# Last buckets of two graph layers: gathered rows and one-hots in place of stored matrices

## The chip, the cores and the metric

One core of a Trainium2 chip runs one program. The metric is device time in microseconds (us) of one execution, the median over runs. Engines are named as in the profile: PE (matrix products) with PEld (its weight loads), DVE (vector), ACT (scalar), POOL (GpSimd), SP (which here only issues DMAs). A bank is one of PE's eight accumulator banks, 128 partitions by 512 f32.

## The reference

A graph of 8192 nodes (32 features each, `x`) and 262144 edges, sorted by target `dst`, so a node has 32 edges on average. Four layers, each followed by a residual sum and a normalization over the 32 features:

```python
def layernorm(x): return (x - mean(x)) / sqrt(var(x) + 1e-5)
def segsum(msg): return segment_sum(msg, dst, 8192)

x = layernorm(x + segsum(einsum('ei,eio->eo', x[src], weight[edge_type])))   # layer 0, 64 types
x = layernorm(x + segsum(x[src] * edge_weight[:, None]))                     # layer 1
x = layernorm(x + segsum(x[src]))                                            # layer 2
x = layernorm(x + L3(x, src, dst, edge_attr_4, edge_attr_32))                # layer 3
```

Layer 3 makes a small matrix for each edge from its 32 attributes (two dense steps) and multiplies it into the source row.

## The kernel before

All the work is in `raw_layers`, written engine by engine with marks and waits: `PE.after(mark)` makes the engine wait for a mark, `V.mark(ins)` makes one. Every engine runs its instructions in the order in which they are written there. Edges lie in 2048 tiles of 128 (edge on partition), eight tiles to a *group*, so 256 groups; nodes lie in 64 *buckets* of 128. Because edges are sorted, group g meets only a window of 128 nodes that begins near node 32 g; four groups hold about one bucket.

**Layer 0 (L607 to L681)** gathers, for each edge, a row of `ytab` (one row per node and edge type, 64 MB, made in the prologue) with an indirect DMA from POOL (`gathers`, `indirect`, L387), one per tile. A one-hot of the target within the group's window (`one_hot`, L508) sums the rows on PE into a bank (L662, in three bf16 parts); `windows` (L483) adds the shifted windows of neighbouring groups into buckets, and `normalize` (L452) ends eight buckets at a time.

While layer 0 waits for its gathers, `matrices(i)` (L553, one call per group or so) builds what layers 1 and 2 need: for each of 256 steps, the adjacency of 32 nodes as dense blocks. DVE makes two one-hots and a weighted copy of the first (L562, L564, L567), PE multiplies them (L576), ACT moves the result out as bf16 counts and f32 weights (L581, L582), and SP stores 1 MB into `famat` (weighted, layer 1) and 0.5 MB into `fcmat` (counts, layer 2).

**Layers 1 and 2 (L756 to L779)** read these matrices back: layer 1 in 32 chunks of two buckets, layer 2 in 16 chunks of four; each chunk is one DMA of 8.4 MB (64 KB for each partition) into one of two buffers. `bring(n)` (L692) issues the load of a chunk once its buffer is free, that is once the products two chunks before have read it. The loop over chunks does, on PE: the 64 products of the chunk (L761 or L764), then `turn` (L733) for the chunk before, which adds partial sums into buckets and, every eight buckets, calls `normalize`; in layer 2 also `self_part` (L720), node-wise products for layer 3. Layer 2 begins after layer 1's last normalization. Layer 2's results are stored to `fxtab` (L480), 1 MB.

**Layer 3 (L842 to the end)** gathers from `fxtab`, again one indirect DMA per tile on POOL, once the stores to `fxtab` have landed. SP's DMAs are all in one queue, and POOL's in another.

Of the kernel before, what the change touches and what calls it, by code (L numbers as in the profile page):

```python
# [101 lines left out]
AW = 41200  # L102


@with_exitstack
def in_order(ctx: ExitStack, tc, x, a, w0, w1, b1, w2, si, keep):


    nc = tc.nc
    dram = ctx.enter_context(tc.tile_pool(name="fdram", bufs=1, space=DRAM))  # L110
    const = ctx.enter_context(tc.tile_pool(name="fconst", bufs=1))
    pool = ctx.enter_context(tc.tile_pool(name="fps", bufs=1, space=PSUM))
    m = {}
    m["ytab"] = dram.tile([N * R, D], FP, name="fytab")
    m["xtab"] = dram.tile([N, D], FP, name="fxtab")
    m["hist"] = dram.tile([GG + 4, 8, 16], FP, name="fhist")

    m["amat"] = dram.tile([P, NU * 512], FP, name="famat")
    m["cmat"] = dram.tile([P, NU * 512], BF, name="fcmat")

    def sb(name, shape, dt=FP):
        m[name] = const.tile(shape, dt, name="f_" + name)

    sb("x_b", [P, NB, D])
    for name, dt in (("src", I32), ("row", I32), ("rel", FP)):
        sb(name, [P, TT], dt)
    sb("ident", [P, P])
    sb("shift", [P, 10 * WS])
    sb("iota_s", [P, P])
    sb("iota_b", [P, 16], BF)  # L130
    sb("stack", [P, D])
    sb("upper", [P, P])
    sb("small", [P, 8])
    sb("lnf", [P, 3, LC * D])
    sb("lns", [P, 4, LC])
    sb("arena", [P, AW])
    m["bank"] = pool.tile([P, 8, 512], FP, name="bank")
    res = keep.tile([P, NB, D], FP, name="x_a")
    m["x_a"] = res
    bad = keep.tile([1, 1], I32, name="bad")  # L140
    with tc.tile_critical():
        raw_layers(tc, x, a, w0, w1, b1, w2, si, m, bad)
    return res, bad


def raw_layers(tc, x, a, w0, w1, b1, w2, si, m, bad):
# [7 lines left out]
    ytab, xtab, hist, amat, cmat = (m[k] for k in ("ytab", "xtab", "hist", "amat", "cmat"))  # L154
# [294 lines left out]
    x_st = Landing(tc, "st_x")  # L449
    ln_last = [None]  # L450

    def normalize(l, c, acc, pm, x_in, x_out, x3=None):  # L452


        ds = slice(c * LC, (c + 1) * LC)
        y, yc, sq = (lnf[:, k].rearrange("p (d f) -> p d f", f=D) for k in range(3))
        V.after(pm, ln_last[0])
        read = own(V, V.e.tensor_add(y, acc.rearrange("p (d f) -> p d f", f=D), x_in[:, ds, :]))  # L458
        own(V, V.e.tensor_reduce(lns[:, 0], y, AX.X, OP.add))
        own(V, V.e.tensor_scalar(lns[:, 1], lns[:, 0], 1.0 / D, None, op0=OP.mult))  # L460
        vm = V.mark(V.e.tensor_sub(yc, y, lns[:, 1, :, None].to_broadcast([P, LC, D])))
        A.after(vm)
        V.after(A.mark(A.e.activation(sq, yc, AF.Square)))
        A.after(V.mark(V.e.tensor_reduce(lns[:, 2], sq, AX.X, OP.add)))
        V.after(A.mark(A.e.activation(lns[:, 0], lns[:, 2], AF.Sqrt, bias=eps, scale=1.0 / D)))
        own(V, V.e.reciprocal(lns[:, 3], lns[:, 0]))
        xo = x_out[:, ds, :]
        ln_last[0] = V.mark(V.e.tensor_tensor(xo, yc, lns[:, 3, :, None].to_broadcast([P, LC, D]), op=OP.mult))
        if x3 is not None:

            r1, r2 = y, sq
            V.after(ln_last[0])
            own(V, V.e.tensor_copy(x3[:, ds, 0:D], xo))
            own(V, V.e.tensor_sub(r1, xo, x3[:, ds, 0:D]))
            own(V, V.e.tensor_copy(x3[:, ds, D:2 * D], r1))
            own(V, V.e.tensor_sub(r2, r1, x3[:, ds, D:2 * D]))
            ln_last[0] = V.mark(V.e.tensor_copy(x3[:, ds, 2 * D:], r2))
        if l == 2:
            S.after(ln_last[0])
            x_st.add(S.e.dma_start(xtab.rearrange("(d p) f -> p d f", p=P)[:, ds, :], xo))  # L480
        return read

    def windows(c, acc, free):  # L483

        d0 = c * LC
        todo = []
        for j in [0, 1, 2, 3, -2, -1, 4]:
            lo, hi = 0, LC
            while 4 * (d0 + lo) + j < 0:
                lo += 1  # L490
            while 4 * (d0 + hi - 1) + j >= GG:
                hi -= 1
            if lo < hi:
                todo.append((j, lo, hi))
        wv = win.rearrange("p (d j) f -> p d j f", j=4)
        PE.after(*free)
        for n, (j, lo, hi) in enumerate(todo):
            g0 = 4 * (d0 + lo) + j
            ins = PE.e.matmul(acc[:, lo * D:hi * D].rearrange("p (d f) -> p d f", f=D),
                              shift[:, P - WS * j:2 * P - WS * j], wv[:, g0 // 4:g0 // 4 + hi - lo, g0 % 4, :],  # L500
                              start=(n == 0), stop=(n == len(todo) - 1))
        return PE.mark(ins)

    def ready(c):

        return min(GG, 4 * (LC * (c + 1) - 1) + 5)
# [46 lines left out]
    def matrices(i):  # L553
# [3 lines left out]
        if i % WB == 0:  # L557
            n = min(WB * 16, CB * 16 - i * 16)
            V.after(now(V))
            own(V, V.e.tensor_copy(w_ps[:, 0:n], meta_w.rearrange("p n k -> p (n k)")[:, i * 16:i * 16 + n]))  # L560
# [3 lines left out]
        V.e.tensor_tensor(oh_l[:, b], iota[:, None, :].to_broadcast([P, 16, P]),  # L564
                          meta_l[:, pp, k0:k0 + 16, None].to_broadcast([P, 16, P]), op=OP.is_equal)
        wo = (i % WB) * 16
        vm = V.mark(V.e.tensor_tensor(oh_k[:, b, :, 1, :], oh_k[:, b, :, 0, :],  # L567
                                      w_ps[:, wo:wo + 16, None].to_broadcast([P, 16, 64]), op=OP.mult))
        PE.after(vm)
        for q in range(4):  # L570
            bk = [2 + (2 * units[0] + h) % 5 for h in range(2)]
            PE.after(*(bank_free[b5] for b5 in bk))
            for j in range(4):
                for h in range(2):
                    hs_ = slice(64 * h, 64 * h + 64)
                    ins = PE.e.matmul(bank[:, bk[h], :].rearrange("p (c s j) -> p c s j", s=64, j=4)[:, :, :, j],  # L576
                                      oh_l[hs_, b, 4 * q + j, :], oh_k[hs_, b, 4 * q + j], start=True, stop=True)
            pm = PE.mark(ins)
            A.after(pm, st_ld[b].mark() if q == 0 and st_ld[b].n else None)
            for h in range(2):  # L580
                A.e.activation(st_c[:, b, q, h], bank[:, bk[h], 0:256], AF.Copy)  # L581
                bank_free[bk[h]] = am = A.mark(A.e.activation(st_a[:, b, q, h], bank[:, bk[h], 256:512], AF.Copy))  # L582
# [3 lines left out]
        st_ld[b].add(S.e.dma_start(amat[:, 2048 * i:2048 * (i + 1)], st_a[:, b].rearrange("p u h c -> p (u h c)")))  # L586
# [57 lines left out]
    for g in range(GG + 2):  # L644
        if g >= 2 and (g - 2) % per == per - 1:
            vm = bank_out((g - 2) // per)
            while done < NB // LC and ready(done) <= g - 1:
                acc = bank[:, (g - 2) // per % 2, 0:LC * D]
                agg_free[(g - 2) // per % 2] = vm = normalize(0, done, acc, windows(done, acc, (vm,)), x_a, x_b)
                done += 1  # L650
# [15 lines left out]
        if g >= FIRST:  # L666
            upto = min(CB, (g - FIRST + 1) * CB // (GG - FIRST - 4))
# [13 lines left out]
    z = cut(NB, D)  # L681
    zx = cut(2, P)
    end = (now(PE), now(V), now(A), *stored)
# [5 lines left out]
    seq = [(1, c) for c in range(32)] + [(2, c) for c in range(16)]  # L689
    land = {}  # L690

    def bring(n):  # L692
        if n < len(seq):
# [3 lines left out]
            if l == 1:  # L697
                land[n] = m_ld[b].add(S.e.dma_start(buf[b], amat[:, c * 16384:(c + 1) * 16384]))
            else:
                land[n] = m_ld[b].add(S.e.dma_start(buf[b].bitcast(BF), cmat[:, c * 32768:(c + 1) * 32768]))  # L700

    bring(0)
    bring(1)
# [14 lines left out]
    own_part = [None]  # L718

    def self_part(j):  # L720
        xv = x_b[:, 4 * j:4 * j + 4, :].rearrange("p d f -> p (d f)")
        u = j % 2
        if j == 0:
# [5 lines left out]
        PE.after(A.mark(A.e.activation(zx[:, u], bank[:, 4 + u, 0:P], AF.Copy)), zf[1 - u])  # L729
        V.after(PE.mark(PE.e.matmul(bank[:, 6, 0:P], zx[:, u], sis, start=True, stop=True)))  # L730
        zf[u] = V.mark(V.e.tensor_add(z[:, 4 * j:4 * j + 4, :].rearrange("p d f -> p (d f)"), bank[:, 6, 0:P], xv))

    def turn(l, c, n, am):  # L733
# [10 lines left out]
        if d0 + nb == LC:  # L744
            out_free[o] = normalize(l, c * nb // LC, bank[:, 2 + o, 0:LC * D], pm, x_b if l == 1 else x_a,
                                    x_a if l == 1 else x_b, x3 if l == 1 else None)
            outs[0] += 1

    for n, (l, c) in enumerate(seq):
        b = n % 2  # L750
        nn = 256 if l == 1 else 512
        if n == 32:
            turn(*pend)
            pend = None
            PE.after(ln_last[0])
# [19 lines left out]
        if l == 2 and c >= 3 and c % 2 == 1:  # L775
            self_part(c - 3)
            self_part(c - 2)
# [3 lines left out]
    self_part(NB // 4 - 2)  # L781
    self_part(NB // 4 - 1)
# [43 lines left out]
    G.after(x_st.mark())  # L826
# [15 lines left out]
    def fetch_rows(q):  # L842

        if q < NQ:
            G.after(quad.get(q - AHEAD, {}).get("w"))
            rows[q // 2] = gathers(xtab, src, q // 8, q % 8 * 4, 4)
# [68 lines left out]
    for q in range(NQ + LAG3 + 2):  # L915
# [69 lines left out]
        if 0 <= c < NQ and c % 2 == 1:  # L985
# [9 lines left out]
            while done < NB // LC and ready(done) <= g + 1:  # L995
                k, wp = w_bank()
                acc = bank[:, 3 + 2 * k, 0:LC * D]
                w_free[k] = normalize(3, done, acc, windows(done, acc, (w_free[k], gm)), z, x_a)
                done += 1
# [471 lines left out]
```

## Time and profile before

| | us |
|---|---|
| median of 10 runs | 6447.62 (6442.39 to 6453.61) |
| the profiled execution | 6447.4 |
| its span | 6445.0 |

Busy time over the span: PE 4779.0, PEld 3442.4, DVE 4362.1, ACT 1755.4, POOL 3975.1 us. The page's strip of 40 slices of 161 us each shows the stages; a digit is a busy share in tenths:

```
PE   7356666565656565644446879999999999999998
DVE  4278878888888897830000017888878888888887
POOL 2677777777777777730000017777777777777775
DMA  9468777777777777889999961111111111111111
```

The first one or two slices are the prologue, up to slice 17 it is layer 0, then layers 1 and 2 until slice 23, and then layer 3.

How the views are read: a group of instructions is `line engine operation out<-in`, with its count and busy time, and what ended the engine's idle time before it. In the chain of waits each step is followed back to what released it, so a piece named DMA is time in which the next step waited for that transfer. POOL's and SP's DMAs are issued by the engine and carried out by 16 DMA engines which all queues share; a DMA queue's row has its packets, MB, and the time that its packets took as a share of 16 engines. The trace also keeps a record of each packet, with queue, size and duration.

### The profile page before, as it was taken

How to read it: one execution, taken by the hardware profiler on the slowest of the kernel's cores; microseconds unless marked ns; L12 is line 12 of the kernel's file. 1: busy time of each engine (PE TensorE's matmuls, PEld its weight loads, DVE VectorE, ACT ScalarE, POOL GpSimd, SP SyncE). 2: the span in 40 equal slices, each digit the busy share in tenths (PEclk: the TensorE clock that was granted, in tenths of full speed). 3: DMA queues.
4: the chain of work that ended last, by engine and by line, in shares of the span. 5: the costliest groups of instructions: out<-in, count | busy, mean ns of one | idle time of the engine just before them, and what ended most of it. 6: DMA issues, size and time to landing. Idle time of an engine off the chain costs nothing.

```text
span 6445.0 us, 89476 instructions
## 1 busy us (share of the span) xinstructions
PE 4779.0 (74%) x34036; PEld 3442.4 (53%) x34036; DVE 4362.1 (68%) x9246; ACT 1755.4 (27%) x4886; POOL 3975.1 (62%) x4174
## 2 busy tenths in 40 slices
PE   7356666565656565644446879999999999999998
PEld 3155555555555555532223446666666666666665
DVE  4278878888888897830000017888878888888887
ACT  5345444454545454510000001111111111111111
POOL 2677777777777777730000017777777777777775
PEclk7577878887878787877777879999999999999999
DMA  9468777777777777889999961111111111111111
GB/s 350 160 140 182 181 169 187 176 187 174 178 174 190 171 190 164 187 276 432 431 425 407 387 242 28 28 28 28 28 28 28 28 28 28 28 28 29 28 29 21
DMA packets 290756, 999.51 MB, mean 155 GB/s; under 512 B 99021, under 2 KB 175886, under 8 KB 250638
## 3 DMA queue, kind: packets, MB, share of 16 engines
q1 hardware_dynamic: 155742, 916.89, 40.1%
q0 software_dynamic: 134144, 73.67, 13.1%
q8 instruction: 272, 4.46, 0.3%
q10 hardware_dynamic: 432, 3.15, 0.2%
q14 instruction: 166, 1.36, 0.1%
HBM read 521.39 MB, written 471.99 MB: 154 GB/s over the span
## 4 chain that ended last, share of the span: by engine, by line
PE 27%; DMA 26%; DVE 20%; POOL 18%; issue 7%; ACT 1%; POOLq 0%; SPq 0%; DVEq 0%; ACTq 0%
POOL f_arena L387 18%; PE bank L932 9%; DMA f_arena<-fytab,f_row 8%; DMA f_arena<-famat 8%; PE bank L923 7%; DMA f_arena<-fxtab,f_src 5%; DVE f_arena L564 5%; DMA f_arena<-fcmat 3%; PE bank L576 3%; DVE f_arena L562 2%; PE bank L761 2%; DVE f_arena L567 2%; DVE f_arena L509 2%; PE bank L764 2%; PE bank L899 2%
## 5 line engine op out<-in xcount | busy, mean ns | idle before, releaser
L387 POOL DMA_INDIRECT f_arena<-fxtab,f_src x2048 | 1950.2, 952 | 1645.0 <-PE bank L730 1021.3
L387 POOL DMA_INDIRECT f_arena<-fytab,f_row x2048 | 1957.0, 956 | 652.4 <-issue 550.7
L576 PE MATMUL bank<-f_arena 64*128 64x128 f32 x16384 | 1349.3, 331 | 759.6 <-DVE f_arena L567 736.0
L576 PEld LDWEIGHTS bank<-f_arena 64*128 64x128 f32 x16384 | 1272.2, 240 | 827.2 <-DVE f_arena L567 774.2
L932 PE MATMUL bank<-f_arena 128*128 128x344 f32 x4096 | 1314.1, 463 | 0.0
L581 ACT ACTIVATE f_arena<-bank 128x256 bf16<-128x256 f32 x2048 | 868.3, 425 | 1228.8 <-PE bank L576 1172.9
L923 PE MATMUL bank<-f_arena 65*128 65x256 f32 x4096 | 1022.0, 393 | 75.6 <-DVE f_arena L967 75.2
L923 PEld LDWEIGHTS bank<-f_arena 65*128 65x128 f32 x4096 | 770.1, 193 | 429.2 <-DVE f_arena L967 147.7
L932 PEld LDWEIGHTS bank<-f_arena 128*128 128x128 f32 x4096 | 800.0, 195 | 360.5 <-issue 33.8
L907 ACT ACTIVATE f_arena<-bank,f_arena 64x512 f32<-64x512 f32 x512 | 351.0, 686 | 2123.7 <-PE bank L899 2117.3
L582 ACT ACTIVATE f_arena<-bank 128x256 f32<-128x256 f32 x2048 | 882.8, 432 | 0.0
L509 DVE TENSOR_TENSOR f_arena<-bank,f_rel 128x512 f32<-128x512 f32 (+1 forms) x768 | 660.5, 860 | 55.8 <-ACT f_arena L541 44.4
L564 DVE TENSOR_TENSOR f_arena<-bank,f_arena 128x2048 f32<-128x2048 f32 x256 | 586.5, 2291 | 8.7
L967 DVE TENSOR_TENSOR f_arena<-bank,f_arena 128x256 f32<-128x256 f32 x1536 | 552.6, 417 | 0.0
L761 PE MATMUL bank<-f_arena,f_x_b 128*32 128x256 f32 x4096 | 295.8, 460 | 338.4 <-DMA f_arena<-famat 338.4
L458 DVE TENSOR_TENSOR f_lnf<-bank,f_x_b 128x256 f32<-128x256 f32 x8 | 3.4, 425 | 611.0 <-PE bank L741 611.0
L761 PEld LDWEIGHTS bank<-f_arena,f_x_b 128*32 128x32 f32 x4096 | 146.0, 132 | 477.0 <-DMA f_arena<-famat 312.7
L863 DVE TENSOR_TENSOR f_arena<-f_arena 128x192 f32<-128x192 f32 x256 | 93.5, 365 | 412.1 <-DMA f_arena<-fxtab,f_src 410.7
L963 DVE TENSOR_TENSOR f_arena<-bank,f_arena 128x512 f32<-128x512 f32 x512 | 349.6, 683 | 0.0
L662 PE MATMUL bank<-f_arena 128*128 128x96 bf16 x2048 | 142.5, 217 | 268.5 <-DVE f_arena L629 268.4
L562 DVE TENSOR_TENSOR f_arena<-bank,f_arena 128x1024 f32<-128x1024 f32 x256 | 312.0, 1219 | 1.1
L624 DVE TENSOR_SCALAR bank<-f_arena 128x256 int32<-128x256 int32 x256 | 107.9, 422 | 301.1 <-DMA f_arena<-fytab,f_row 300.4
(133 smaller groups left out, 3763.4 us busy)
## 6 DMA issues: line engine op xcount, KB each, us to landing
famat<-f_arena SPq DMA_DIRECT2D x256, 1024.0 KB
fcmat<-f_arena SPq DMA_DIRECT2D x256, 512.0 KB
fytab<-f_arena SPq DMA_DIRECT2D x64, 1024.0 KB, 11.4
f_arena<-fytab,f_row POOLq DMA_INDIRECT x2048
f_arena<-fxtab,f_src POOLq DMA_INDIRECT x2048
f_arena<-laid_ea SPq DMA_DIRECT2D x64, 512.0 KB, 3.6
f_arena<-laid_ea SPq DMA_DIRECT2D x64, 64.0 KB
f_arena<-laid_xT ACTq DMA_DIRECT2D x1, 1024.0 KB, 8.3
```

What stands on the lines that cost most here:

```text
L387: return G.e.indirect_dma_start(out=dest, out_offset=None, in_=table, in_offset=bass.IndirectOffsetOnAxis(ap=ix, axis=0))
L509: return V.e.tensor_tensor(o, iota[:, None, :].to_broadcast([P, n, P]), rel[:, t:t + n, None].to_broadcast([P, n, P]), op=OP.is_equal)
L562: own(V, V.e.tensor_tensor(oh_k[:, b, :, 0, :], iota[:, None, 0:64].to_broadcast([P, 16, 64]), meta_k[:, pp, k0:k0 + 16, None].to_broadcas ...
L564: V.e.tensor_tensor(oh_l[:, b], iota[:, None, :].to_broadcast([P, 16, P]), meta_l[:, pp, k0:k0 + 16, None].to_broadcast([P, 16, P]), op=OP ...
L576: ins = PE.e.matmul(bank[:, bk[h], :].rearrange("p (c s j) -> p c s j", s=64, j=4)[:, :, :, j], oh_l[hs_, b, 4 * q + j, :], oh_k[hs_, b, 4 ...
L581: A.e.activation(st_c[:, b, q, h], bank[:, bk[h], 0:256], AF.Copy)
L582: bank_free[bk[h]] = am = A.mark(A.e.activation(st_a[:, b, q, h], bank[:, bk[h], 256:512], AF.Copy))
L761: ins = PE.e.matmul(bank[q * D:(q + 1) * D, b, 0:256].rearrange("p (u h j) -> p u h j", h=2, j=4), x_b[:, s, :], mv[:, s], start=(s < 4), ...
L907: quad[q + h] = dict(h=A.mark(A.e.activation(hs[0:64, (q + h) % 4], bank[64 * h:64 * h + 64, 2, :], AF.Relu, bias=b1_s[64 * h:64 * h + 64])))
L923: ins = PE.e.matmul(wp[:, t, :], hs[0:65, q % 4, t * P:(t + 1) * P], w2_s[0:65], start=True, stop=True)
L932: ins = PE.e.matmul(bank[:, g % 2, 0:MW], oh[:, c % NO, t, :], p[:, c % NP, t, :], start=(c % 2 == 0 and t == 0), stop=(c % 2 == 1 and t = ...
L967: ins = V.e.tensor_tensor(pq[:, :, 128 + 64 * mm:192 + 64 * mm].rearrange("p t (o i) -> p t o i", i=8), wp[:, :, 192:256].rearrange("p t ( ...
```

## The change

Layer 1's last 10 buckets and layer 2's last 4 are no longer computed from matrices. Layer 1 has 27 chunks and layer 2 has 15. For the rest, groups 214 to 255 in layer 1 and 238 to 255 in layer 2, POOL gathers the source rows from the result of the layer before (42 x 8 and 18 x 8 indirect DMAs), DVE scales them by the edge weight in layer 1, and PE sums them with one-hots. For that, every layer's result goes to a table of its own in DRAM. `matrices` makes 240 steps instead of 256, and the weighted half only in the first 216. Each chunk's load is issued as eight DMAs of 8 KB for each partition.

The helpers take a first bucket and a count in place of a number of eight buckets, `normalize` stores its result in layers 0, 1 and 2, and `windows` can read a ring of 24 groups:

```diff
+HB = {1: 10, 2: 4}
+MADE = {l: CB - 4 * HB[l] for l in (1, 2)}
-    m["xtab"] = dram.tile([N, D], FP, name="fxtab")
+    m["xtabs"] = [dram.tile([N, D], FP, name=f"fxtab{l}") for l in range(3)]
...
-        if l == 2:
+        if l < 3:
             S.after(ln_last[0])
-            x_st.add(S.e.dma_start(xtab.rearrange("(d p) f -> p d f", p=P)[:, ds, :], xo))
+            x_st[l].add(S.e.dma_start(xtabs[l].rearrange("(d p) f -> p d f", p=P)[:, ds, :], xo))
...
+        both = i < MADE[1]
...
-        vm = V.mark(V.e.tensor_tensor(oh_k[:, b, :, 1, :], oh_k[:, b, :, 0, :],
-                                      w_ps[:, wo:wo + 16, None].to_broadcast([P, 16, 64]), op=OP.mult))
+        if both:
+            vm = V.mark(V.e.tensor_tensor(oh_k[:, b, :, 1, :], oh_k[:, b, :, 0, :],
+                                          w_ps[:, wo:wo + 16, None].to_broadcast([P, 16, 64]), op=OP.mult))
...
-            upto = min(CB, (g - FIRST + 1) * CB // (GG - FIRST - 4))
+            upto = min(MADE[2], (g - FIRST + 1) * MADE[2] // (GG - FIRST - 4))
...
-    z = cut(NB, D)
+    HG = {l: 4 * (NB - HB[l]) - 2 for l in (1, 2)}
+    RING = 24
+    hoh = cut(3, 4, P)
+    hx = cut(4, GT, D)
+    hwin = cut(RING, D)
+    ew = cut(TT - T1)
+    z = row.bitcast(FP).rearrange("p (d f) -> p d f", f=D)
...
-    seq = [(1, c) for c in range(32)] + [(2, c) for c in range(16)]
+    chunks = {1: (NB - HB[1]) // 2, 2: (NB - HB[2]) // 4}
+    seq = [(l, c) for l in (1, 2) for c in range(chunks[l])]
...
-            if l == 1:
-                land[n] = m_ld[b].add(S.e.dma_start(buf[b], amat[:, c * 16384:(c + 1) * 16384]))
-            else:
-                land[n] = m_ld[b].add(S.e.dma_start(buf[b].bitcast(BF), cmat[:, c * 32768:(c + 1) * 32768]))
+            for k in range(8):
+                o = buf[b][:, 2048 * k:2048 * (k + 1)]
+                if l == 1:
+                    land[n] = m_ld[b].add(S.e.dma_start(o, amat[:, c * 16384 + 2048 * k:c * 16384 + 2048 * (k + 1)]))
+                else:
+                    land[n] = m_ld[b].add(S.e.dma_start(o.bitcast(BF), cmat[:, c * 32768 + 4096 * k:c * 32768 + 4096 * (k + 1)]))
     bring(0)
+    ew_in = load(S, "ld_ew", ew, a["ew"][:, T1:])
     bring(1)
```

The self parts go to a list and run one chunk after the normalization that they need, in the banks of their transposes instead of a bank that both share. What is new is the gathering, the sums, and their turn at the end of each chunk:

```diff
+    def h_fetch(l, g):
+        if g >= GG:
+            return
+        k = count["got"] % 4
+        count["got"] += 1
+        G.after(x_st[l - 1].mark() if g == HG[l] else None, hx_free[k], hl.get((l, g - 2), (0, None))[1])
+        for t in range(GT):
+            mk = h_ld[k].add(indirect(hx[:, k, t, :], xtabs[l - 1][:, :], src[:, g * GT + t:g * GT + t + 1]))
+        hl[l, g] = k, mk
+
+    def h_sums(l, g0, n):
+        PE.after(h6_free[0])
+        for g in range(g0, g0 + n):
+            k, landed = hl[l, g]
+            V.after(landed)
+            if l == 1:
+                V.after(ew_in)
+                V.e.tensor_tensor(hx[:, k], hx[:, k], ew[:, g * GT - T1:(g + 1) * GT - T1, None].to_broadcast([P, GT, D]), op=OP.mult)
+            for hh in range(2):
+                r = count["oh"] % 3
+                count["oh"] += 1
+                V.after(hoh_free[r])
+                PE.after(V.mark(one_hot(hoh[:, r], g * GT + 4 * hh, 4)))
+                for t in range(4):
+                    ins = PE.e.matmul(bank[:, 6, (g - g0) * D:(g - g0 + 1) * D], hoh[:, r, t, :], hx[:, k, 4 * hh + t, :],
+                                      start=(hh == 0 and t == 0), stop=(hh == 1 and t == 3))
+                hoh_free[r] = hx_free[k] = PE.mark(ins)
+            h_fetch(l, g + 4)
+        V.after(now(PE))
...
+    def h_turn(l, upto):
+        while h_at[l] < upto:
+            n = min(4, upto - h_at[l])
+            h_sums(l, h_at[l], n)
+            h_at[l] += n
+            d = h_done[l]
+            nd = min(4, NB - d)
+            if nd and ready(d + nd) <= h_at[l]:
+                acc = bank[:, 6, 256:256 + nd * D]
+                h6_free[0] = finished(l, d, nd, acc, windows(d, nd, acc, (h6_free[0],), hwin, RING))
+                h_done[l] += nd
 
     for n, (l, c) in enumerate(seq):
...
-        if n == 32:
-            turn(*pend)
-            pend = None
-            PE.after(ln_last[0])
+        if c == 0:
+            if l == 2:
+                turn(*pend)
+                pend = None
+                h_turn(1, GG)
+                PE.after(ln_last[0])
+            h_at[l], h_done[l] = HG[l], NB - HB[l]
+            for k in range(4):
+                h_fetch(l, HG[l] + k)
...
         if pend:
             turn(*pend)
-        if l == 2 and c >= 3 and c % 2 == 1:
-            self_part(c - 3)
-            self_part(c - 2)
+        for j in z_todo:
+            self_part(j)
+        z_todo[:], z_next[:] = z_next, []
+        h_turn(l, HG[l] + (GG - HG[l]) * c // (chunks[l] - 1))
         pend = (l, c, n, am)
```

The end of `h_sums`, left out here, copies the sums from the bank into the ring `hwin`; `finished` is `normalize` with the layer's inputs and outputs, and notes the self parts that have become possible. So the groups of a layer's rest are spread evenly over its chunks, and four groups are gathered ahead, each not before the second group before it has landed.

## The prediction

> **What bounds the kernel now.** I read the busy time by stretches first, then the waits, the DMA queues by stretch, the chain of waits around the stages, and the timeline of the second layer. The stretches: layer 1's matrices (2820 to 3457 us), layer 2's with the ends around them (3457 to 3827), layer 3 (3827 to the end), layer 0 (237 to 2790).
>
> ```profile
> 2820.00:3457.00 637.00, 302.71 (x4088) 156.82 (x4088) 29.55 (x84) 17.79 (x45) 0.00 (x0) 0.71 1.00 426
> 3457.00:3827.00 370.00, 284.84 (x1336) 160.54 (x1336) 28.66 (x84) 21.67 (x51) 0.00 (x0) 0.86 0.91 360
> 3827.00:6445.00 2618.00, 2492.19 (x9328) 1645.69 (x9328) 2095.37 (x6269) 356.75 (x528) 1950.15 (x2048) 0.96 0.15 28
> 237.00:2790.00 2553.00, 1523.69 (x18590) 1408.82 (x18592) 2123.12 (x2690) 1236.18 (x4130) 1935.40 (x2026) 0.80 0.73 171
> ```
>
> Columns: stretch, length, busy us of PE, PEld, DVE, ACT and POOL, the granted clock, the DMA share, GB/s. In layer 1 DMA is at 1.00 and POOL at zero. Layers 0 and 3 are POOL's: 2048 gathers each, one start every 1.25 us in the timeline (0.94 us busy, 0.30 of issue).
>
> ```profile
> POOL f_arena L387 <- PE bank L730: 1021.3, 1, 1021.3
> POOL f_arena L387 <- issue: 1086.1, 3564, 0.3
> SPq L586 <- ACT f_arena L582: 2316.1, 256, 155.2
> ```
>
> POOL has one long wait, between its last gather of layer 0 (2805.8) and its first of layer 3 (3827.04). Anything done before it begins is hidden under POOL; so is everything after it. This change is worth what it does to those 1021 us. Inside, loads set the pace:
>
> ```profile
> 2877.11 30.35 DMA f_arena<-famat
> 2907.51 10.12 PE bank L761 x128
> 2917.64 28.54 DMA f_arena<-famat
> 2946.22 9.54 PE bank L761 x128
> ```
>
> These pairs are every second chunk (two buffers): 39 us for two. The first load is issued at 2819.66, the 32nd has landed at 3457.24: 637.6 us, 19.9 a chunk. Layer 2's first product starts at 3476.68, its last at 3801.17: 15 steps of 21.6 us, against 16.7 of PE:
>
> ```profile
> 3758.08 16.68 PE L764 MATMUL bank<-f_arena 128*96 128x512 bf16 x64 [8.48 <-DMA f_arena<-fcmat]
> ```
>
> **Layer 0, nothing.** 16 matrices go whole and 24 more lose their weighted half. On DVE that is 16 x (1.22 + 2.29 + 1.21) + 24 x 1.21 = 105 us (rows L562, L564 and L567), and some on ACT and PE. All of it lies under POOL's 2581 us, which keep every gather. Eight new stores of the layer's result stand in SP's queue, each behind a DVE mark, ahead of matrix stores; SP already waits 2316 us there for ACT. Without that cover matrix stores would be late, and then ACT, which refills their buffers.
>
> **Layer 1's loads.** 27 chunks for 32: 27 x 19.9 = 538 us at today's price. Each load is cut in eight, so packets shrink from 64 KB to 8 KB. In the packet records the 64 KB reads have a median of 2421 ns, 302.6 for 8 KB. The program's opening loads (15 to 21 us) are 8 KB reads with all 16 engines full, and take 313 ns. I take that: x 1.034 = 556 us. The ends: 302.6 (538 us; no less, since the shortest 8 KB packet takes 309 and the shortest 64 KB one 2415), and 349, the mean of the 8 KB stores into the same table in layer 0 (538 x 1.153 = 620). SP issues eight for one, 0.3 us each: 2.6 us, under the other buffer's 20 us load. Without that cover the engines would stand still for it.
>
> The Trainium skill speaks against this part: "DMA: Bandwidth & Descriptors", "Latency and other measured facts", has copies of 16 KiB rows slowed at large power-of-two row pitches, 164 GB/s at 2 MiB where 214 is full. Famat's pitch is 2 MiB (1024 x 512 x 4 bytes), yet the trace reads it at 426 GB/s with 64 KB packets, so for those the row contradicts the page. An estimate by that page's ratio would add some 170 us in layer 1 and 85 in layer 2, for about 6685.
>
> **Layer 1's gathers.** 42 groups of 8 = 336 gathers. POOL: 336 x 1.25 = 420 us, inside 597 (below) in which it does nothing today. DMA: the gather queue's packets,
>
> ```profile
> q0 software_dynamic: 50915, 26.17, 9.6%
> q0 software_dynamic: 25592, 13.15, 22.0%
> ```
>
> (packets, MB, share of 16 engines), are from 4000 to 6000 us (1592 gathers of layer 3) and from 1000 to 2000 (802 of layer 0): 0.096 x 2000 / 1592 = 121 ns a gather on each engine, and 274 ns. By packet record a gather is one 1 KB packet and one of 4 bytes (9 ns) on each engine. Layer 3's 1 KB packet, same table size as here, has a median of 59 and a mean of 91 with 16 to 32 load packets beside it; that is the nearest row, so 100 ns: 34 us. Ends: 62 (53 ns, the mean with fewer than eight other gather packets near, and 9; 21 us in all) and 274 (92 us). Do they come in time? With a load packet of 313 ns let in before each of a group's 16 packets, a group takes 16 x 313 + 8 x 100 = 5.8 us on an engine, less than POOL's 10. A chunk of 22 us uses 1.6 groups and four slots are ahead. DVE waits for each group's landing, and behind that wait stand the next normalization and PE's sums; four slots, some 50 us, cover it.
>
> **Layer 1's other work.** The new stores of its result are 8192 packets of 128 bytes at 13 ns: 6.7 us of each engine. DVE, 30 us busy of 637, takes 42 x (0.42 + 2 x 0.68) = 75 us more (a 128x256 product, a 128x512 one-hot). PE takes 16 small passes a group at 0.14 us (eight take 0.97 to 1.24 us at L741): 3.6 us a chunk, on 10 of 20. Both lie beside the loads. The 172 KB of edge weights between the first two loads are 0.4 us. Sum: 556 + 34 + 7 = 597 us for 637.6: 41 less.
>
> **Between the layers.** Today the first product of layer 2 starts 19.4 us after the last landing of layer 1 (products, bucket sums, a normalization with its three-part copy). Now the gathered rest of the last buckets and their own normalization stand ahead of that: sums of two groups 4.5, windows 2.5, normalization 4, on PE and then DVE: 11 us. Two loads are under way meanwhile, so only what outlasts them counts: the load that needs the first buffer goes out 46 us after the landing instead of 36, when the other's load has ended at 40. I take 5 us. The last store of layer 1's result sits on SP's queue behind those loads and lands about 41; POOL's first gathers of layer 2 wait for it and need 10, and the sums want them at 63. Cover: 12 us.
>
> **Layer 2.** 15 chunks, 14 steps. By DMA: 21.63 x 1.034 + 144 gathers x 0.1 / 15 = 23.3 us a step. By PE: products 16.7, bucket sums 0.8, self parts 0.95 (1.9 every second chunk), 18 / 14 groups x 2.25 = 2.9, and waits for DVE: every second chunk a normalization (3.5, from 3792.79 to 3796.27) stands ahead of a one-hot (0.68) on DVE, 2.1 on average, in the others an addition, 0.5. The self parts now run a chunk after their normalization and in banks of their own; their count is the same, and `z` in the memory of `row` costs nothing, as nothing reads `row` after layer 0. Sum 23.95. So PE passes the loads by a little: 24.0 x 14 = 336 us for 324.5. If DVE's waits hide, 22.2 (the cheap ends of the loads); with 8 KB at 349 it is 25.9 (21.63 x 1.153 + 1), with gathers at 274 it is 25.
>
> **Into layer 3.** The end today: bucket sums, two self parts, a normalization and the store that POOL waits for, from 3816.8 to 3827.04: 10.2 us. Now the gathered end comes first: sums of two groups 4.5, copy and windows 3, a normalization of 3.5 that the last matrix buckets' normalization queues behind, less the 2 us of self parts that no longer lie in between: 19 us.
>
> **The sum.** Before: 637.6 + 19.4 + 324.5 + 15.6 + 10.2 = 1007.3 us from the first load to the first gather of layer 3. After: 597 + 24.4 + 336 + 15.6 + 19 = 992. That is 15 less. The profiled execution took 6447.4 us, 2.4 more than its span, and stands at the median of 6447.62. I predict 6432. Layer 1 gains 41 us, and layer 2 gives back 25: its one chunk less is worth no more than its gathers.
>
> **Rivals.**
>
> 1. Dear pieces (slower). 8 KB reads of a table with such a pitch cost what its 8 KB stores do, 349 ns: 64 more in layer 1, 14 x 1.9 = 27 in layer 2: 6523. For it: those stores' mean is 15% above their floor, and the layer 2 reads are already 9% over theirs (mean 2631). Against: the 313 of the opening reads. It decides from some 322 ns up (27 x 64 packets x 9 ns = 16 us).
> 2. Dear or late gathers (slower). At layer 0's 274 ns: 336 x 0.174 = 58 more, and 14 in layer 2: 6504. For it: layer 0's gathers share engines with streams, as these will. Against: those read a 64 MB table, these 1 MB. A PE stall on landings would have the same effect and would show as DVE waiting for fxtab.
> 3. All the cheap ends: loads at 302.6 (18 less), gathers at 62 (13 less), DVE's waits hidden (14 x 1.8 = 25 less): 6376.
>
> **How the numbers follow.** Forecast 0.50, about 6410 to 6455; dear pieces 0.18; dear or late gathers 0.20; cheap ends 0.12. What a measurement can't tell from no change is 0.2%, 13 us: faster is below 6434.7, slower above 6460.5. The forecast gives 0.32 faster, 0.16 same, 0.02 slower, so faster 0.44, same 0.16, slower 0.40. The range runs from the cheap ends, 6380, to dear pieces, 6530; both dear cases together (6595) stay outside.
>
> **What would show it.** Right: POOL busy some 320 us in layer 1 and 137 in layer 2; first load to 27th landing near 597 us at a DMA share of 1.00; 8 KB packets near 313 ns and gather packets near 91; layer 2's steps near 24 us with PE waiting for DVE's one-hots rather than for fcmat. Wrong: PE or DVE waiting for fxtab landings in layer 1, a DMA share below 0.95 there, 8 KB packets over 322 ns, or a length of layers 0 or 3 that differs by more than 5 us.

## The result, and the profile after

The changed kernel takes 6759.13 us (median of 8 runs, 6749.39 to 6760.16) beside 6447.62 for the kernel before in the same set (6445.88 over all 28 of its runs): a ratio of 1.0483, interval 1.0474 to 1.0492. In two of the five sets of runs told below the kernel before itself took 7510 us (the 7510 us sets), so a ratio is always against the kernel before of the same set. The profiled execution took 6756.23 us, its span 6754.5. That is slower, and outside the predicted range. The busy time by stretches of the kernel after (layer 1's matrices, layer 2's with the ends, layer 3, layer 0; columns as before):

```profile
2862.00:3743.00 881.00, 357.77 (x4243) 231.42 (x4235) 102.47 (x248) 16.23 (x42) 290.17 (x306) 0.65 0.98 258
3743.00:4136.00 393.00, 327.26 (x1485) 212.03 (x1481) 56.81 (x153) 21.46 (x52) 135.99 (x144) 0.82 0.83 320
4136.00:6754.00 2618.00, 2486.98 (x9336) 1642.92 (x9336) 2097.81 (x6271) 357.32 (x530) 1950.00 (x2048) 0.96 0.15 28
237.00:2790.00 2553.00, 1519.31 (x17578) 1412.90 (x17578) 2024.76 (x2619) 1117.96 (x3687) 1935.40 (x2026) 0.75 0.66 153
```

Layers 0 and 3 have their old lengths. The loss is in layer 1: the DMA engines are as full as before (0.98), but move 258 GB/s where they moved 426. A full engine with less to show for it means dearer packets, not a wait. The waits of layer 1 in the kernel after (engine, line, what it waited for: total us, times, longest) agree:

```profile
PE bank L859 <- DMA f_arena<-famat: 527.7, 27, 44.1
...
POOL f_arena L389 <- PE bank L815: 461.2, 24, 42.7
DVE f_arena L517 <- PE bank L815: 297.0, 15, 33.8
...
POOL f_arena L389 <- DMA f_arena<-fxtab,f_src: 1.2, 4, 0.3
```

PE waits for every one of its 27 loads. POOL and DVE, which bring the gathered rows, wait for PE's sums, which stand in line behind those loads. Nobody waits for gathered rows to speak of (1.2 us), so the gathers are neither late nor dear. The chain of waits of the kernel after, where the pairs of before were (start, length, what):

```profile
3151.97 42.66 DMA f_arena<-famat
3194.67 9.40 PE bank L859 x128
3214.27 6.93 SPq L723
3221.25 42.08 DMA f_arena<-famat
3263.37 9.19 PE bank L859 x128
```

Two chunks, one of each buffer, now take 68.7 us (3194.67 to 3263.37) instead of 39. SP's sequencer has entered the chain: the eight issues of a load of `famat` keep it for 20.1 us in the median, and 5.9 at least. The engines are full meanwhile (0.98), so this can cost little of its own.

The DMA queues of the kernel after in that stretch (packets, MB, share of 16 engines) say whose packets fill the engines:

```profile
q1 hardware_dynamic: 37836, 221.96, 95.4%
q0 software_dynamic: 9900, 5.08, 2.4%
```

The gather queue holds 2.4%. By the packet records, the 8 KB packets read from `famat` take 494 ns on average, the 1 KB gather packets 58. In layer 2 the same 8 KB pieces, read from `fcmat`, take 328. The tables differ in their rows: 2 MiB for each partition in `famat`, 1 MiB in `fcmat`.

### The profile page after: what moved, and what is told of

It is laid out like the page before. It is cut to its first block, busy times and chain, and to the rows that moved or that the text cites. A ratio compares the mean times of both kernels' runs of the same rounds, so it can differ in the third digit from the quotient of the medians.

```text
span 6754.5 us, 88484 instructions
## 1 busy us (share of the span) xinstructions
PE 4866.4 (72%) x33318; PEld 3569.9 (53%) x33318; DVE 4364.9 (65%) x9404; ACT 1634.0 (24%) x4438; POOL 4429.4 (66%) x4654
## 4 chain that ended last, share of the span: by engine, by line
PE 29%; DMA 25%; POOL 19%; DVE 16%; issue 7%; SPq 3%; ACT 1%; POOLq 0%; DVEq 0%; ACTq 0%
POOL f_arena L389 19%; DMA f_arena<-fytab,f_row 9%; DMA f_arena<-famat 9%; PE bank L1031 8%; PE bank L1022 7%; DMA f_arena<-fxtab,f_src 5%; DVE f_arena L573 3%; PE bank L587 3%; PE bank L862 3%; SPq L723 3%; PE bank L859 2%; DVE f_arena L571 2%; DVE f_arena L577 2%; DVE f_arena L517 2%; PE bank L998 2%
## 5 line engine op out<-in xcount | busy, mean ns | idle before, releaser
L389 POOL DMA_INDIRECT f_arena<-fxtab,f_src x2528 | 2404.4, 951 | 1499.1 <-issue 650.5
L587 PE MATMUL bank<-f_arena 64*128 64x128 f32 (+1 forms) x15360 | 1333.4, 346 | 717.4 <-DVE f_arena L577 686.0
L592 ACT ACTIVATE f_arena<-bank 128x256 bf16<-128x256 f32 x1920 | 789.0, 416 | 1335.3 <-PE bank L587 1325.7
L517 DVE TENSOR_TENSOR f_arena<-bank,f_rel 128x512 f32<-128x512 f32 (+1 forms) x888 | 738.7, 836 | 419.1 <-PE bank L815 324.6
L594 ACT ACTIVATE f_arena<-bank 128x256 f32<-128x256 f32 x1728 | 738.0, 427 | 0.0
L859 PE MATMUL bank<-f_arena,f_x_b 128*32 128x256 f32 x3456 | 246.1, 455 | 527.7 <-DMA f_arena<-famat 527.7
L573 DVE TENSOR_TENSOR f_arena<-bank,f_arena 128x2048 f32<-128x2048 f32 x240 | 549.8, 2291 | 8.2
L859 PEld LDWEIGHTS bank<-f_arena,f_x_b 128*32 128x32 f32 x3456 | 121.9, 131 | 643.0 <-DMA f_arena<-famat 487.3
L676 PE MATMUL bank<-f_arena 128*128 128x96 bf16 x2048 | 151.2, 225 | 316.6 <-DVE f_arena L643 316.4
L868 ACT ACTIVATE f_arena<-bank 128x256 f32<-128x256 f32 (+1 forms) x42 | 20.8, 496 | 1185.6 <-PE bank L859 865.8
L676 PEld LDWEIGHTS bank<-f_arena 128*128 128x128 bf16 x2048 | 109.9, 107 | 356.2 <-DVE f_arena L643 304.8
```

Source lines behind the costliest of these rows:

```text
L389: return G.e.indirect_dma_start(out=dest, out_offset=None, in_=table, in_offset=bass.IndirectOffsetOnAxis(ap=ix, axis=0))
L517: return V.e.tensor_tensor(o, iota[:, None, :].to_broadcast([P, n, P]), rel[:, t:t + n, None].to_broadcast([P, n, P]), op=OP.is_equal)
L573: vm = V.mark(V.e.tensor_tensor(oh_l[:, b], iota[:, None, :].to_broadcast([P, 16, P]), meta_l[:, pp, k0:k0 + 16, None].to_broadcast([P, 16 ...
L592: ins = A.e.activation(st_c[:, b, q, h], bank[:, bk[h], 0:256], AF.Copy)
L594: ins = A.e.activation(st_a[:, b, q, h], bank[:, bk[h], 256:512], AF.Copy)
L859: ins = PE.e.matmul(bank[q * D:(q + 1) * D, b, 0:256].rearrange("p (u h j) -> p u h j", h=2, j=4), x_b[:, s, :], mv[:, s], start=(s < 4), ...
```

## The experiments

All kernels compute the whole reference.

**Pieces alone.** The kernel before, with its loads cut in eight and nothing else:

```diff
-                land[n] = m_ld[b].add(S.e.dma_start(buf[b], amat[:, c * 16384:(c + 1) * 16384]))
...
+            for k in range(8):
+                o = buf[b][:, 2048 * k:2048 * (k + 1)]
...
+                    land[n] = m_ld[b].add(S.e.dma_start(o, amat[:, c * 16384 + 2048 * k:c * 16384 + 2048 * (k + 1)]))
```

> The kernel before, with each chunk's load cut into eight DMAs of 8 KB for each partition, and nothing else of the change: no gathers, all 32 and 16 chunks. Three theories of why layer 1's 8 KB packets took 495 ns in the changed kernel instead of 313. (Pitch) 8 KB reads of rows 2 MiB apart slow each other: packets near 495 ns here too, layer 1 near 32 x 64 x 0.495 = 1014 us instead of 638, in all about 6830 us. (Pieces) eight DMAs for one are slow by themselves, through their issue: the same time here, so this run doesn't part it from the pitch. (Gathers) the gathers slow the loads beside them: packets near 313 ns, layer 1 near 660, in all about 6480 us.

Measured: 6744.3 us, ratio 1.0474 (1.0448 to 1.0500). No row is gathered, and nearly the whole loss is there, with 32 chunks to load where the changed kernel has 27. That parts the gathers from the loads. It is less than the 6830 us expected of the pitch, as the packets took 440 ns and not 495. Its stretches, layer 1's products and then layer 2's:

```profile
2856.00:3769.00 913.00, 313.80 (x4212) 161.84 (x4211) 29.52 (x84) 17.76 (x45) 0.00 (x0) 0.65 0.98 291
3780.00:4103.00 323.00, 265.99 (x1172) 149.91 (x1173) 21.03 (x62) 18.06 (x41) 0.00 (x0) 0.91 0.95 387
```

POOL is at zero in both. Layer 1 runs at 291 GB/s with full engines (440 ns a packet); layer 2, with the same piece size, at 387 (317 ns), and takes 333.7 us from the last product of layer 1 to its own last one, 349.6 before. So it is neither the piece size by itself nor the number of DMAs, which are the same in both layers: it is the pieces in layer 1's table.

**Large loads.** The changed kernel with each load whole again, that is the gathers alone (the reverse of the edit above).

> The changed kernel with each chunk loaded by one DMA of 64 KB for each partition, as before; the gathers stay. If the engines alternate between queues packet by packet, each of a group's 16 packets waits for one of 2.4 us: 39 us a group, 42 groups 1640 us in layer 1, in all about 7500 us, with POOL waiting for landings. If gather packets slip in without such waits, layer 1 is 538 + 336 x 0.066 + 7 = 567 us, layer 2 as in the changed kernel, in all about 6420 us, and then the pieces were not needed.

Measured: 6593.14 us, ratio 1.0239 (1.0219 to 1.0260). The 64 KB packets take 2611 ns in layer 1 (2444 before). Its waits in layer 1:

```profile
DVE f_arena L806 <- DMA f_arena<-fxtab,f_src: 406.6, 22, 42.0
POOL f_arena L389 <- DMA f_arena<-fxtab,f_src: 333.8, 29, 28.3
...
PE bank L813 <- DVE f_arena L517: 305.4, 21, 35.8
...
PE bank L857 <- DMA f_arena<-famat: 69.1, 6, 31.2
```

Here gathered rows do come late: POOL waits up to 28 us for a landing, DVE up to 42, and PE for DVE's one-hots (L517), which stand behind DVE's wait. The DMA engines stand idle for a sixth of the time (a share of 0.83), as loads wait for PE and PE for rows. It misses both numbers expected: gather packets are neither held up by a whole load packet each time, nor do they pass freely. So the pieces have a use: they let gather packets through, as the 1.2 us above shows. And they have a price.

**Another row length.** The changed kernel with `famat` made only as wide as the 216 steps that are stored, 1728 KB a row, once with 4 KB added and once without:

```diff
-    m["amat"] = dram.tile([P, NU * 512], FP, name="famat")
+    m["amat"] = dram.tile([P, MADE[1] * 2048 + 1024], FP, name="famat")
```

> The changed kernel with famat's rows 216 x 8 KB + 4 KB = 1732 KB apart instead of 2048 KB; the table has as many columns as are written, and 4 KB more. Pitch: layer 1's 8 KB packets near 313 ns, its loads 27 x 64 x 0.313 = 541 us plus 22 for gathers and 7 for stores, 570 to 590 instead of 906, in all about 6435 us. Pieces (issue of eight DMAs for one): unchanged, about 6759 us with packets near 495 ns. Gathers: unchanged, about 6759.

> The changed kernel with famat's rows 216 x 8 KB = 1728 KB apart, no padding; the pitch is a multiple of 64 KB but not a power of two. If the pitch matters and only powers of two are bad: packets near 313 ns, about 6435 us. If any large round pitch is bad: between 313 and 495 ns, between 6435 and 6759 us. Pieces or gathers: about 6759.

Measured: 6427.57 us for both (10 and 8 runs), ratio 0.9983 (0.9974 to 0.9993, and 0.9972 to 0.9993). The instructions and the bytes that they move are those of the changed kernel; only addresses differ, in `famat` and perhaps in tables that lie behind it. It came out as expected of the pitch. The stretches of the one with 1732 KB, layer 1's products, layer 2's, and layer 0:

```profile
2845.00:3417.00 572.00, 356.98 (x4242) 231.78 (x4234) 102.22 (x248) 16.20 (x42) 301.46 (x318) 0.73 1.02 399
3433.00:3780.00 347.00, 303.19 (x1361) 191.24 (x1361) 40.64 (x100) 16.98 (x39) 135.89 (x144) 0.85 0.88 343
...
237.00:2790.00 2553.00, 1552.76 (x17580) 1450.95 (x17581) 2029.87 (x2620) 1123.04 (x3687) 1935.54 (x2026) 0.75 0.47 153
```

Layer 1 goes from 881 to 572 us at 399 GB/s. In layer 0, where the table is written, the same 153 GB/s now take a share of 0.47, and not 0.66 as in the changed kernel or 0.59 as in the run with large loads, which is of the same set. The 4 KB more are not what matters: 1728 KB without them does the same. The 8 KB packets of layer 1, in ns:

| kernel | row of `famat` | 5% | 25% | 50% | 75% | 95% | mean |
|---|---|---|---|---|---|---|---|
| after | 2 MiB | 309 | 309 | 388 | 614 | 946 | 494 |
| pieces alone | 2 MiB | 309 | 309 | 313 | 566 | 808 | 440 |
| 1732 KB, 1728 KB | 1.69 MiB | 309 | 313 | 315 | 322 | 412 | 327 |

The shortest are the same; with the 2 MiB row a quarter and more take about double.

**How small is too small?** 16 KB pieces (four a load) of the 2 MiB rows; and `famat` as two tables of 1 MiB rows, with 8 KB pieces. Both ran first in the two 7510 us sets:

```diff
-            for k in range(8):
-                o = buf[b][:, 2048 * k:2048 * (k + 1)]
+            for k in range(4 if l == 1 else 4):
...
+                    o = buf[b][:, 4096 * k:4096 * (k + 1)]
...
```

```diff
+    m["amat"] = [dram.tile([P, 128 * 2048], FP, name=f"famat{k}") for k in range(2)]
...
```

> The changed kernel with famat split into two tables of 128 steps, so that rows lie 1024 KB apart: a power of two as well, half as large. If every large power of two is bad, packets in layer 1 stay well over 400 ns and the time near 6750 us. If it is the 2 MiB that is bad (layer 2's table has 1 MiB rows, and its 8 KB packets took 317 ns in the run with pieces alone): packets near 327 ns and about 6428 us, as with 1728 KB.

> The changed kernel, famat's rows 2 MiB apart as in it, with four pieces of 16 KB for each partition instead of eight of 8 KB. If the slowing is a matter of how often an engine jumps from row to row, it falls with the size: 64 KB packets were 1% over their floor and 8 KB ones 60%, so 16 KB some 20 to 30% over 605 ns, layer 1 about 90 us longer than with 1728 KB rows, in all 6500 to 6560 us. If every piece under 64 KB suffers alike: packets near 970 ns, about 6750 us. Without any effect of the pitch at this size: about 6430 us.

> The changed kernel with famat in two tables with rows 1024 KB apart, once more for the same reason. If the 2 MiB of the pitch is what is bad and not each large power of two: 8 KB packets near 327 to 342 ns and about 6428 us; else packets over 400 ns and up to 6750 us.

> The changed kernel, rows 2 MiB apart, with 16 KB pieces, once more for the same reason. The first trial's packets took 684 ns where 626 are without the pitch's effect (+9%), on a chip whose loads were not the bound. Where they are: 740 ns and 6500 to 6560 us if the effect falls with the size; 970 ns and 6750 us if all small pieces suffer alike; 6430 us without an effect.

Ratios there: two tables 1.0076 (1.0057 to 1.0094) and 1.0084 (1.0066 to 1.0103); 16 KB 1.0058 (1.0040 to 1.0077) and 1.0060 (1.0042 to 1.0078). They don't tell the loads apart, since layer 1 is not bound by them there (the last experiment shows by what). The packets do: 342 ns in both for 8 KB of a 1 MiB row, 684 and 687 for 16 KB of a 2 MiB row. Layer 0 of these runs is a further test, as the two versions do the same there and `famat` has the same size in all: between 1000 and 2400 us a 4 KB store into `fcmat` takes 310 to 319 ns with 2 MiB rows and 164 to 165 with two tables (162 to 163 with 1728 KB). So it is the length of the rows and not the size in all. The 16 KB pieces were then run in the set in which the kernel before takes 6447.82:

> The changed kernel, rows 2 MiB apart, with 16 KB pieces. Where the kernel before takes 6440 us: packets near 740 ns and 6500 to 6560 us if the effect falls with the size of a piece; 970 ns and 6750 us if all small pieces suffer alike. Where it takes 7510: packets near 685 ns again, PE being the bound.

Measured: 6441.36 us (8 runs), ratio 0.9991 (0.9980 to 1.0001), below both numbers expected of it and near the 6430 us that the expectations of the earlier trials had for no effect. Its layer 1:

```profile
2847.00:3435.00 588.00, 363.12 (x4245) 233.53 (x4246) 102.72 (x248) 16.40 (x43) 300.11 (x317) 0.71 1.00 391
```

391 GB/s with 2 MiB rows; a 16 KB packet takes 663 ns, where two of 8 KB at 1728 KB take 654. So in these reads the penalty needs both the row length and the small piece, and most of it goes between 8 and 16 KB.

**Which part of the change pays.** With 1728 KB rows, layer 2 was left to matrices entirely; then also two more buckets of layer 1 were gathered, which makes the rows 1664 KB:

```diff
-HB = {1: 10, 2: 4}
+HB = {1: 10, 2: 0}
...
```

```diff
-HB = {1: 10, 2: 4}
+HB = {1: 12, 2: 0}
...
```

> The changed kernel with 1728 KB rows, and layer 2 left with all its 16 chunks of matrices (no gathers and no store of layer 1's result; layer 1 keeps its 10 gathered buckets). My account has layer 2 lose by the change: from the end of layer 1's products to layer 3's first gather 387 us with gathers, 344 in the run with pieces alone. So 43 us less: about 6385 us, faster than both kernels by some 0.9%. If layer 2's loss lay in the way from layer 1 to layer 2 and not in its gathers, about 6410 us or more.

> The run before with 12 gathered buckets in layer 1 instead of 10: 26 chunks, 50 groups. While layer 1 is set by its loads: a chunk of 21 us less, 64 gathers at 56 ns more, 17 us less: about 6368 us. POOL needs 500 us of some 570. If the sums at the end of each chunk (1.9 groups) or POOL's look-ahead of four groups already bind, no gain or a loss: 6385 us or more, with DVE waiting for fxtab.

> The changed kernel with 1728 KB rows, and layer 2 left with all its 16 chunks of matrices, once more: the chip of the first trial ran the kernel before in 7510 us, so its stages are not those of the account. On a chip where the kernel before takes 6440: from the end of layer 1's products to layer 3's first gather 344 us instead of 387, about 6385 us, ratio 0.991. If layer 2's loss lay in the way from layer 1 to layer 2 and not in its gathers: about 6410 us or more.

> The run before with 12 gathered buckets in layer 1, once more for the same reason. While layer 1 is set by its loads 17 us less than with 10: about 6368 us. If the sums at the end of each chunk or POOL's look-ahead already bind, as they seem to on the chip of the first trial (85 us more than with 10): 6385 us or more.

In the 7510 us sets: 1.0081 (1.0068 to 1.0095) and 1.0093 (1.0077 to 1.0108) for matrices in layer 2; 1.0203 (1.0189 to 1.0217) and 1.0212 (1.0198 to 1.0226) with twelve buckets. The longest waits of PE in a run with matrices in layer 2 there:

```profile
PE bank L587 <- ACT f_arena L594: 485.0, 290, 28.2
PE bank L676 <- issue: 333.3, 517, 9.2
...
PE bank L860 <- issue: 131.9, 155, 2.4
```

"Issue" is time in which PE waited for nothing that the profile shows, and `L676` and `L860` are layer 0's sums and layer 1's products. Layer 1's products take 701 us there, and 572 in the run of the same kernel below, where PE's wait at `L860` is 198.3 us for `famat` and none for issue. The 8 KB packets take 332 ns: the loads are as cheap, but PE's issue sets the pace. Why it is slower there, and why twelve buckets cost some 90 us more, was not settled; that the change's added work on PE is no longer hidden would fit, but wasn't tried. In the set in which the kernel before takes 6447.82:

> The changed kernel with 1728 KB rows, and layer 2 left with all its 16 chunks of matrices. Where the kernel before takes 6440 us: from the end of layer 1's products to layer 3's first gather 344 us instead of 387, about 6385 us, ratio 0.991, if layer 2's loss lies in its gathers; about 6410 us or more if it lies in the way from layer 1 to layer 2. Where the kernel before takes 7510: slower than it by 0.9% again, since PE's issue binds.

> The run before with 12 gathered buckets in layer 1. Where the kernel before takes 6440 us and loads set layer 1: 17 us less than with 10, about 6368 us; if the sums at the end of each chunk or POOL's look-ahead bind: 6385 us or more. Where it takes 7510: some 85 us more than with 10 again.

Measured: 6389.52 us, ratio 0.9907 (0.9891 to 0.9924), and 6377.68, 0.9892 (0.9876 to 0.9909). The stretches of the first, layers 1 and 2:

```profile
2846.00:3418.00 572.00, 362.50 (x4243) 233.91 (x4235) 102.38 (x248) 16.20 (x42) 300.99 (x318) 0.73 1.02 401
3433.00:3759.00 326.00, 265.43 (x1174) 149.56 (x1174) 21.06 (x62) 18.06 (x41) 0.00 (x0) 0.90 0.95 379
```

Layer 1 keeps its gain, layer 2 drops from 347 to 326 us, and the way into layer 3 shrinks too (24.6 us to 10.3). From the end of layer 1's products to layer 3's first gather it is 351 us, for 387 with layer 2's gathers and 344 expected. In the 7510 us sets the same version lost 0.8 to 0.9%. With twelve buckets layer 1's products take 559 us, 13 less where 17 were expected; it is the fastest version measured: its four runs (6374.83 to 6380.13 us) lie below the other's four (6384.97 to 6390.76).

## Why the prediction was wrong

The five terms of its sum, from the first load to the first gather of layer 3, in us:

| term | before | predicted | after | 1728 KB rows |
|---|---|---|---|---|
| first load issued to last landing of layer 1 | 637.6 | 597 | 911.7 | 588.2 |
| to the first product of layer 2 | 19.4 | 24.4 | 24.6 | 24.5 |
| steps of layer 2 | 324.5 | 336 | 336.7 | 332.0 |
| its last chunk's products | 15.6 | 15.6 | 16.8 | 16.8 |
| to the first gather of layer 3 | 10.2 | 19 | 24.7 | 24.6 |
| sum | 1007.3 | 992 | 1314.5 | 986.1 |

One term fails. It is 314.7 us too short, and the whole sum 322.5.

**The step that failed** is the price of a piece: "The program's opening loads (15 to 21 us) are 8 KB reads with all 16 engines full, and take 313 ns. I take that", with 349 as the dear end. It measured 494. The pieces of layer 1 then take 27 chunks x 64 packets x 0.494 = 854 us of each engine, where the sum had 556: 298 of the 314.7 us missed. The rest is for the most part engines not quite full (892 us of packets in the 911.7).

The opening loads read other tables; I moved a price from one row length to another. And I took it from the end of them alone. The same loads in the ten microseconds before, in the kernel before:

```profile
5.00:10.00 5.00, 0.00 (x0) 0.00 (x0) 0.66 (x4) 0.00 (x0) 1.58 (x5) 1.00 1.05 272
10.00:15.00 5.00, 0.00 (x0) 0.00 (x0) 0.00 (x0) 0.00 (x0) 0.00 (x0) 1.00 0.96 238
15.00:21.00 6.00, 5.87 (x24) 2.39 (x24) 4.60 (x3) 3.75 (x5) 0.00 (x0) 1.00 1.02 425
```

The engines were as full, at 238 to 272 GB/s, and by the packet records an 8 KB packet took some 510 ns on average from 5 to 15 us. So the trace did hold a warning that 313 is no fixed price for 8 KB. Why these packets are dear at first is not known; 2 MiB rows it cannot be, as no input read there is larger than 1 MB. The row of `famat` itself that I had, 64 KB packets near their floor, holds for its piece size only. And the stores into the table, 15% over their floor, I took for the size of the effect, which was another size in reads.

**Rival 1**, dear pieces, had the mechanism, and said where it would be seen: 8 KB packets over 322 ns. Its price of 349 was too low by 145 ns, and it was put on layer 2 as well, where the packets kept to 328 (the 1 MiB rows). The Trainium skill had pointed at the row length, in "DMA: Bandwidth & Descriptors", "Latency and other measured facts": its row on row pitches of large powers of two. I set it aside on the strength of the 64 KB packets and the opening reads. By its ratio I had estimated some 6685 us; 6759 was measured, so the estimate was near, but partly by luck: its 85 us in layer 2 put the ratio for 2 MiB on rows of 1 MiB, which cost nothing of the kind, and layer 1's 170 were little more than half of the 315 by which its loads came out longer. Its figure is for copies of 16 KiB rows from one HBM table to another; this case's reads show hardly any loss with 16 KB pieces (663 ns for 654), while at 8 KB they show 494 for 327, more than its 2 MiB figure. Its advice is to pad the row. A padded 2 MiB row was not run here; rows of 1728, 1732 and 1664 KB, and of 1 MiB for the packets, took the loss away.

**Rival 2**, dear or late gathers: no. Gather packets took 58 ns in layer 1 (47 with 1728 KB rows), below the 91 I took and near the cheap end of 53. Four slots were enough beside 8 KB pieces (1.2 us of POOL's waits); rows come late only with 64 KB loads.

**Rival 3**, cheap ends: the gathers were cheap, the loads were not.

**What held.** Layer 0 cost nothing, nor did the stores in SP's queue, nor layer 3. The way between the layers and layer 2's step (24.0 predicted, 24.05 measured; between 3758 and 4112 us PE waits 31.9 us for DVE's one-hots and 12.2 for `fcmat`, as said) were right. With 1728 KB rows the kernel takes 0.9983 of the time before, against 0.9976 predicted (6432 of 6447.62). By the table layer 1 gains some 50 there, and layer 2 and its ends give back 28. The table sets profiles of two sets side by side, whose kernels before differ by 9 us (6447.62 and 6438.69); within its set this kernel is 11 us faster, for 15 predicted. Luck has a part in layer 1's 588 for 597: the loads were 9 us dearer than the sum had them (327 ns a packet, 565 us for 556), and the gathers some 15 us cheaper. The way into layer 3 was 5.7 us short: 24.7 measured for 19. The eight issues of a load took SP 20.1 us in the median and not 2.6 (7.9 with 1728 KB rows), under cover as said.

**Open.** What in the memory makes 2 MiB rows dear was not tried. Nor is it known why the packets take 494 ns beside gathers and 440 without: in a stretch of 25 us with no gather packet (2990 to 3015) they took 505 as well. The two runs are of different sets, and the effect differed between these in layer 0 too, where no gathers of this change run: 8 KB stores took 350 ns in the one and 332 to 333 in the other. Two tables of 1 MiB rows were not run where loads set the pace.

## What to carry to other kernels

A packet's price belongs at least to its size and its table's row length together: take it from a row of the trace that has both, over the whole of the loads and not their best stretch, and where none has, run the loads alone before anything is built on them. A row of 2 MiB was cheap to avoid; here the same instructions with 1728 KB for 2 MiB a row took 4.8% less (0.9983 over 1.0483). When engines are full but GB/s fall, look at packet durations by size and quantile, and not for a wait.

## What the runs showed of the hardware

- **The row length taxes others' packets too.** With 2 MiB rows, between 1000 and 2000 us in layer 0, a 1 KB gather packet from `ytab` took 270 ns and a 4 KB store into `fcmat` 274 (266 and 263 in the kernel before). In the set of the run with 1732 KB rows it was 215 and 242 with 2 MiB (large loads) and 130 and 170 with 1732 KB, though the rows of `ytab` and `fcmat` are the same. I had put those 266 down to the 64 MB table. It costs no time, as POOL sets layer 0's pace.
- **8 KB reads of 1 MiB rows are not dear**: 312 to 313 ns in the median at all three places where they were seen (`fcmat` in layer 2, with gathers and without, and the two tables). Their neighbours may still pay: in the 7510 us sets gather packets of layer 0 took 226 to 231 ns with two tables, 254 to 262 with 2 MiB rows and 143 to 155 with 1728 KB.
